# One context loop split in two, two early transposes placed behind the feed-forward, and the loads of c in odd steps, in a fused cross-attention layer

## The chip, the cores and the metric

The kernel runs on one core of a Trainium2 chip. The metric is the device time of one execution in microseconds (us). Before the change it is 1655.78 us, the median of three runs (1654.61 to 1656.57).

## The reference

One transformer layer with cross attention: `x` gives the queries, `c` (the input `ctx_1024`) gives keys and values. Both are 128 sequences of 128 tokens with 256 features, all in 32-bit floating point. There are 16 heads of 16 features. A token attends only to the tokens strictly before it, and the attention row of the first token is set to zero.

```python
q = (query @ Wq + bq).reshape(b, s, N_HEADS, D_K).transpose(0, 2, 1, 3)
k = (key @ Wk + bk).reshape(b, s, N_HEADS, D_K).transpose(0, 2, 1, 3)
v = (values @ Wv + bv).reshape(b, s, N_HEADS, D_K).transpose(0, 2, 1, 3)
scores = jnp.einsum('bhqd,bhkd->bhqk', q, k) / jnp.sqrt(jnp.float32(D_K))
allowed = j < i + mask                     # mask is 0
scores = jnp.where(allowed, scores, NEG_INF)
attn = jax.nn.softmax(scores, axis=-1)
attn = attn.at[:, :, 0, :].set(0.0)
ctx = jnp.einsum('bhqk,bhkd->bhqd', attn, v)
attn_out = ctx @ Wo + bo
x = layer_norm(query + attn_out, ln1_g, ln1_b)
ffn = jax.nn.relu(x @ W1 + b1) @ W2 + b2   # 256 -> 1024 -> 256
out = layer_norm(x + ffn, ln2_g, ln2_b)
```

## The kernel before, in words

The work is cut into 64 pairs of sequences, numbered p = 0 to 63. The instructions of TensorE (PE), VectorE (DVE), ScalarE (ACT) and GpSimd (POOL) stand in the order in which the code emits them. Only the DMA queue of SyncE (SP) is ordered by a planner of the framework, which may place a load ahead of an older transfer. [...]

Pairs 0 and 1 have an order written out by hand. From p = 2 on a loop runs, and this text calls one turn of it a step. Step p does the scores and the softmax of pair p, the context and the output projection of pair p-1, the projections of pair p+1, the transposes of the inputs of pair p+2, and feed-forward work of older pairs. On PE, a step is in this order:

1. `scores(p, 1)`, the high half of the query rows (L333), into two double banks of PSUM. The masks on DVE (L350) read them, and `maximum`, `exponential` and `sums` follow on DVE, POOL and ACT.
2. The first feed-forward unit. A unit is half of the hidden layer (`hidden`, L611) or one sequence of the second layer (`second` at L627, or `second_alone` at L639 with a bank of its own). Each is 16 matrix instructions in the trace, since a 32-bit product is made of two.
3. `scores(p, 0)`, the low half.
4. The second feed-forward unit.
5. `weigh(p-1)`, the context: products of the transposed attention weights `pT` with `vd` (low rows, L443) and `vz` (high rows, L451), 48 products or 96 matrix instructions together. Each writes a strip of 32 partitions, and four strips run side by side. `context` copies the result (ACT, L463).
6. The projections: `queries` (L267), `attention_out` (L470), `keys` (L267), `values` (L299).
7. In steps 2 to 5 `turn_x1_on_pe(p-1)`: four transposes on PE (L233) of the normalised rows `x1` of pair p-1, copied by ACT (L601). From step 6 on `turn_x1` does this with a transpose on DVE (L585) and transfers over DRAM on SP (`across`, L247).
8. The last units. From step 7 on they are both halves of `hidden(p-2)`; steps 2 to 6 take their units from a table, `plan`.

`weigh` needs `pT`. In the loop `turn(p)` makes it: three transposes on DVE (L399), then 16 transfers on the SP queue (L409), each from one block of 32 partitions to another. Blocks 0 and 1 of `pT` belong to the first sequence of a pair and blocks 2 and 3 to the second, so the products of one sequence need 8 of the transfers. PE waits for these through eight semaphores. The framework spreads these waits: it puts four instructions that only wait (two semaphores each but one) ahead of the first product of each sequence, and the last wait sits on that product's weight load itself. The pairs 0, 1 and 63 get `pT` from PE and ACT instead (`turn_on_pe`), without these waits.

`x1` of pair p-1 comes from a chain within step p: the masks, then maxima, sums and transposes on DVE, with POOL and ACT between, then `attention_sum`, the two `tokens` transposes and `norm1` (L508).

PSUM has four single banks for everything but the scores. A new tile takes the bank that was released longest ago, and PE waits until its last reader has finished.

`load` (L92) brings `x` and `c` of two pairs into buffers with four transfers each; `load_tokens` (L99) brings `x` of two pairs once more, by rows. In an even step p the three come for the pairs p+4 and p+5, after `add_bo`. `tokens(p + 2)` reads the loaded buffers in each step (DVE, L252).

Of the kernel before, what the change touches and what calls it, by code (L numbers as in the profile page):

```python
# [13 lines left out]
P = 128  # L14
# [5 lines left out]
def tile_cross_attention_block(  # L20
# [26 lines left out]
    H = 16  # L47
# [6 lines left out]
    NP = B // 2  # L54
# [22 lines left out]

    blocks_of, tokens_of = {}, {}

    def load(ps):  # L80

        n = len(ps)
        for which, src in (("x", x), ("c", c)):
            t = loads.tile(
                [P, KC, n * 2 * NS, 32], F32, tag=f"{which}b{n}", name=f"{which}b_{ps[0]}",
                bufs=n,
            )
            blocks = src[2 * ps[0] : 2 * ps[0] + 2 * n].rearrange(
                "b (i t) (k j f) -> j t k (b i) f", t=32, k=KC, f=32
            )  # L90
            for j in range(NS):
                nc.sync.dma_start(t[32 * j : 32 * j + 32], blocks[j])  # L92
            for u, p in enumerate(ps):
                blocks_of[which, p] = t[:, :, u * 2 * NS : (u + 1) * 2 * NS]

    def load_tokens(g, us=slice(0, 4)):
        if g not in tokens_of:
            tokens_of[g] = loads.tile([P, 4, D], F32, tag="x", name=f"x_{g}")
        nc.sync.dma_start(  # L99
            tokens_of[g][:, us], x[4 * g + us.start : 4 * g + us.stop].rearrange("b p d -> p b d")  # L100
        )
# [118 lines left out]
    def bank(name):  # L220
        return ps_1.tile([P, 512], F32, tag="ps1", name=name)
# [5 lines left out]
    def transposed(src, name):  # L227

        pt = bank(name)
        for k in range(KC):  # L230
            for s in range(2):
                at = (2 * k + s) * P
                nc.tensor.transpose(  # L233
                    pt[:, at : at + P], src[:, s, k * P : (k + 1) * P], ident
                )
        return pt
# [195 lines left out]
    def weigh(p):  # L432

        st = states[p]
        pT = st.pop("pT")
        pc = bank(f"pc_{p}")

        for m in range(KC):
            for s in range(2):
                at = (m * 2 + s) * P  # L440
                blocks = slice(2 * s, 2 * s + 2)
                for j in range(NS):
                    nc.tensor.matmul(  # L443
                        pc[32 * j : 32 * j + 32, at : at + HP],
                        st["vd"][:, s, 4 * m + j].rearrange("p e d -> p (e d)"),
                        pT[:, blocks, H + 2 * j + m, :],
                        start=True, stop=True,
                    )
                for e in range(2):
                    for j in range(NS):  # L450
                        nc.tensor.matmul(  # L451
                            pc[32 * j : 32 * j + 32, at + HP : at + P],
                            st["vz"][:, s, 4 * m + j, 2 * e : 2 * e + 2, :].rearrange(
                                "p e d -> p (e d)"
                            ),
                            pT[:, blocks, 4 * j + 2 * m + e, :],
                            start=(e == 0), stop=(e == 1),
                        )
        st["pc"] = pc
# [133 lines left out]
    def turn_x1_on_pe(p):  # L593
        st = states[p]
        x1T = ffn.tile([P, NS, 4 * 32], F32, tag="x1T", name=f"x1T_{p}")
        st["x1T"] = x1T.rearrange("p i (s k a) -> p s i k a", s=2, k=KC)
        pt = transposed(st["x1"], f"ptn_{p}").rearrange(
            "p (k s i a) -> p k s i a", k=KC, s=2, i=NS
        )
        for k in range(KC):  # L600
            nc.scalar.copy(st["x1T"][:, :, :, k, :], pt[:, k])  # L601

    def hidden(p, fs):
        st = states[p]
        if fs[0] == 0:
            st["hT"] = ffn.tile([P, FC, TP], F32, tag="hT", name=f"hT_{p}")
        for f in fs[::2]:
            ph = bank(f"ph_{p}_{f}")
            for i in range(2):
                for k in range(KC):  # L610
                    nc.tensor.matmul(  # L611
                        ph[:, i * TP : (i + 1) * TP].rearrange("p (s i a) -> p s i a", s=2, a=32),
                        w1[:, k, (f + i) * P : (f + i + 1) * P], st["x1T"][:, :, :, k, :],
                        start=(k == 0), stop=(k == KC - 1),
                    )
            for i in range(2):
                nc.scalar.activation(  # L617
                    st["hT"][:, f + i, :], ph[:, i * TP : (i + 1) * TP], AF.Relu,
                    bias=b1e_c[:, f + i : f + i + 1], scale=1.0,
                )  # L620
# [11 lines left out]
    def second_alone(p, s):  # L632

        st = states[p]
        if "t2" not in st:
            st["t2"] = ffn.tile([P, 2, D], F32, tag="t2", name=f"t2_{p}")
        py = bank(f"py_{p}_{s}")
        for f in range(FC):
            nc.tensor.matmul(  # L639
                py[:, :D], st["hT"][:, f, s * P : (s + 1) * P], w2[:, f, :],  # L640
                start=(f == 0), stop=(f == FC - 1),
            )
        st["py", s] = py
# [27 lines left out]
    def feed(units):  # L671
        for what, p, part in units:
            if what == "hidden":
                hidden(p, range(part * FC // 2, (part + 1) * FC // 2))
            elif p in alone:
                second_alone(p, part)
            else:
                second(p, part)

    def sum_up(units):  # L680

        done = []
        for what, p, part in units:
            if what == "second":
                if p in alone:
                    sum_alone(p, part)
                elif part == 1:
                    second_sum(p)
                if part == 1:
                    done.append(p)  # L690
        return done

    alone = (2, 3)

    def both(what, p):
        return [(what, p, 0), (what, p, 1)]
# [61 lines left out]
    for which in "xc":  # L758
# [9 lines left out]


    plan = {  # L770
        2: ([("hidden", 0, 1)], both("second", 0), both("hidden", 1)),
        3: ([("second", 1, 0)], [("second", 1, 1)], [("hidden", 2, 0)]),
        4: ([("hidden", 2, 1)], [("second", 2, 0)], [("second", 2, 1)]),
        5: ([("hidden", 3, 0)], [("hidden", 3, 1)], [("second", 3, 0)]),
        6: ([("second", 3, 1)], [("hidden", 4, 0)], [("hidden", 4, 1)]),
    }
    waiting, late = [], []
    for p in range(2, NP):
        soon, end = p + 1 < NP, p == NP - 1
        first, then, finally_ = plan.get(  # L780
            p, ([("second", p - 3, 0)], [("second", p - 3, 1)], both("hidden", p - 2))
        )
        scores(p, 1)
        mask(p, 1, 0)
        maximum(p, 1, ONE)
        feed(first)
        mask(p, 1, 1)
        maximum(p, 1, TWO)
        scores(p, 0)
        mask(p, 0, 0)  # L790
        mask(p, 0, 1)
        exponential(p, 1, ONE)
        maximum(p, 0, ALL)
        exponential(p, 1, TWO)
        feed(then)
        sums(p, 1, ONE)
        sums(p, 1, TWO)
        summed = late + sum_up(first + then)
        exponential(p, 0, ALL)
        sums(p, 0, ALL)  # L800
        for q in waiting:
            finish(q)
        weigh(p - 1)
        context(p - 1)
        if soon:
            queries(p + 1)
        attention_out(p - 1)
        if not end:
            turn(p)
        attention_sum(p - 1)  # L810
        if soon:
            keys(p + 1)
        if p + 2 < NP:
            for which in "xc":
                tokens(p + 2, which)
        norm1(p - 1)
        if p > 5:
            turn_x1(p - 1)
        if soon:
            values(p + 1)  # L820
            values_out(p + 1)
        for q in waiting:
            store(q)
        if p <= 5:
            turn_x1_on_pe(p - 1)
        residual1(p - 1)
        for q in summed:
            stats(q, states[q]["t2"], 2)
        if soon:
            add_bo(p + 1)  # L830
        if p % 2 == 0 and p + 4 < NP:
            load([p + 4, p + 5])
            load_tokens(p // 2 + 2)
        for q in summed:
            scale_and_shift(q)
        feed(finally_[:1])
        if end:
            turn_on_pe(p, 1, range(4))
        feed(finally_[1:])
        late = sum_up(finally_)  # L840
        for q in summed:
            norm2(q)
        waiting = summed

    p = NP - 1
# [89 lines left out]
```

## Time and profile before

| What | Value |
|---|---|
| median of three runs | 1655.78 us |
| the profiled execution, its own time | 1652.77 us |
| its span, first to last instruction | 1651.0 us |
| PE busy | 1615.4 us (98%), 16524 matrix instructions |
| DVE, POOL, ACT busy | 1312.6, 1275.4, 766.9 us (80%, 77%, 46%) |
| mean granted clock of TensorE | 0.995 |
| a step in the middle of the run, from scores to scores | 24.77 us |
| the last steps from the table: 3, 4, 5 and 6 | 25.71, 26.67, 26.67, 21.35 us |

An engine's busy time is the time in which one of its instructions ran, as a share of the span. Matrix instructions overlap in the pipeline, so their durations are longer than the distance from one start to the next; distances are what add up to time. `PEld` is the loading of weights, which overlaps with the products. In a timeline each row has its start and its length in us, the engine, the line in the code, the tiles, and in brackets how long the engine had been idle before and what ended that.

### The profile page before, as it was taken

To read this page: it belongs to the slowest core of one execution; us is meant where nothing else is said; L and a number is where in the kernel's file an instruction comes from. 1 tells how busy PE (TensorE), PEld (TensorE's weight loads), DVE (VectorE), ACT (ScalarE), POOL (GpSimd) and SP (SyncE) were. 2 spreads that over 40 slices of the span, in tenths; PEclk is the share of its full clock that TensorE was granted. 3 is DMA by queue.
4 is the path that set the end of the run, shared out by engine and by line. 5 is a ranking of instruction groups with operands and counts; after the bars stand their busy time and mean duration, and the time that the engine had idled before them with its cause. 6 is when DMAs were issued, how large, how long until landed. Compare 5 with 4: busy or idle time off the path is not lost.

```text
span 1651.0 us, 41181 instructions
## 1 busy us (share of the span) xinstructions
PE 1615.4 (98%) x16524; PEld 1342.8 (81%) x16524; DVE 1312.6 (80%) x1983; ACT 766.9 (46%) x1505; POOL 1275.4 (77%) x1108
## 2 busy tenths in 40 slices
PE   7998999999999999999999999999999999999997
PEld 5777888888888888888888888888888888888876
DVE  4767888888888888888888888888888888888852
ACT  4544444444444444444444444444444444444442
POOL 4766878878878878878878878878878878878873
PEclk9999999999999999999999999999999999999999
DMA  8444456566556566655666556565656575556330
GB/s 162 88 104 100 104 138 136 127 151 133 129 128 135 130 148 134 125 133 135 129 146 135 127 130 136 130 146 128 134 134 133 130 149 128 126 134 133 92 87 19
DMA packets 478973, 208.28 MB, mean 126 GB/s; under 512 B 352064, under 2 KB 447296, under 8 KB 478784
## 3 DMA queue, kind: packets, MB, share of 16 engines
q1 hardware_dynamic: 394192, 180.72, 50.3%
q10 hardware_dynamic: 84592, 24.93, 6.2%
q8 instruction: 131, 2.15, 0.6%
q14 instruction: 58, 0.48, 0.1%
HBM read 69.22 MB, written 31.98 MB: 61 GB/s over the span
## 4 chain that ended last, share of the span: by engine, by line
PE 89%; DVE 5%; POOL 3%; issue 1%; DMA 1%; ACT 1%; SPq 1%; ACTq 0%; POOLq 0%; DVEq 0%
PE py L627 25%; PE ph L611 25%; PE pq L267 7%; PE pss L333 7%; PE pk L267 6%; PE pv L299 6%; PE po L470 6%; PE pc L451 3%; PE pc L443 3%; DVE sm L350 1%; DVE nmx L361 1%; POOL sm L383 1%; POOL sm L362 1%; PE py L639 1%; SPq L409 1%
## 5 line engine op out<-in xcount | busy, mean ns | idle before, releaser
L362 POOL TENSOR_TENSOR sm<-sm,nmx 128x1024 f32<-128x1024 f32 x192 | 364.3, 1898 | 219.4 <-DVE nmx L361 219.4
L611 PE MATMUL ph<-x1T,w 128*128 128x256 f32 x2048 | 454.5, 379 | 2.5 <-ACT x1T L601 2.5
L627 PE MATMUL py<-w,hT 128*128 128x256 f32 x1952 | 453.5, 385 | 0.0
L611 PEld LDWEIGHTS ph<-x1T,w 128*128 128x128 f32 x2048 | 388.3, 190 | 57.4 <-ACT x1T L601 3.5
L627 PEld LDWEIGHTS py<-w,hT 128*128 128x128 f32 x1952 | 361.0, 190 | 76.8 <-ACT hT L617 21.9
L350 DVE TENSOR_TENSOR sm<-pss,neg 128x1024 f32<-128x1024 f32 (+1 forms) x256 | 237.9, 950 | 212.6 <-PE pss L333 199.2
L369 ACT ACTIVATE sm<-sm 128x1024 f32<-128x1024 f32 x192 | 203.0, 1057 | 354.0 <-POOL sm L362 344.6
L383 POOL TENSOR_TENSOR sm<-sm,rs 128x1024 f32<-128x1024 f32 x192 | 359.2, 1898 | 2.6 <-DVE rs L382 2.4
L617 ACT ACTIVATE hT<-ph,b1e_c 128x256 f32<-128x256 f32 x512 | 214.1, 470 | 193.5 <-PE ph L611 159.6
L399 DVE STREAM_TRANSPOSE tb<-sm 128x1024 f32<-128x1024 f32 x183 | 220.4, 1231 | 32.2 <-POOL sm L383 22.3
L361 DVE TENSOR_REDUCE nmx<-sm 128x8 f32<-128x1024 f32 (+1 forms) x192 | 234.3, 1220 | 6.6
L381 DVE TENSOR_REDUCE su<-sm 128x8 f32<-128x1024 f32 (+1 forms) x192 | 229.6, 1196 | 1.0 <-ACT sm L369 0.8
L289 ACT ACTIVATE kT<-pk,bkh,half 128x256 f32<-128x256 f32 x256 | 123.6, 563 | 161.7 <-PE pk L267 161.7
L267 PE MATMUL pq<-xT,wq 128*128 128x256 f32 x512 | 130.8, 399 | 3.2 <-ACT xT L669 3.2
L333 PE MATMUL pss<-kT,qT 32*64 32x256 f32 (+1 forms) x4096 | 126.7, 335 | 1.7 <-ACT kT L289 1.3
L470 PE MATMUL po<-wo,cxT 128*128 128x256 f32 x512 | 121.3, 379 | 1.7 <-ACT cxT L463 1.2
L516 POOL TENSOR_TENSOR x1b<-x,g_r 128x512 f32<-128x512 f32 x64 | 81.3, 1271 | 53.7 <-DVE x L508 53.7
L267 PE MATMUL pk<-cT,wk 128*128 128x256 f32 x512 | 121.1, 379 | 1.0 <-ACT cT L669 1.0
L299 PE MATMUL pv<-wv,cT 128*128 128x256 f32 x512 | 121.1, 379 | 0.0
L333 PEld LDWEIGHTS pss<-kT,qT 32*64 32x64 f32 x4096 | 76.3, 131 | 49.1 <-issue 40.6
L267 PEld LDWEIGHTS pq<-xT,wq 128*128 128x128 f32 x512 | 94.2, 194 | 20.3 <-ACT xT L669 3.6
L470 PEld LDWEIGHTS po<-wo,cxT 128*128 128x128 f32 x512 | 97.1, 190 | 15.3 <-ACT cxT L463 1.4
(82 smaller groups left out, 1765.8 us busy)
## 6 DMA issues: line engine op xcount, KB each, us to landing
pT<-tb SPq DMA_DIRECT2D x976, 96.0 KB, 2.2
out_dram<-t ACTq DMA_DIRECT2D x63, 256.0 KB, 3.4
xb<-in_x_dram SPq DMA_DIRECT2D x124, 128.0 KB, 3.8
cb<-in_ctx_dram SPq DMA_DIRECT2D x124, 128.0 KB, 4.7
x<-in_x_dram SPq DMA_DIRECT2D x31, 512.0 KB, 4.7
x1t<-tbx SPq DMA_DIRECT2D x232, 64.0 KB, 1.8
x1T<-x1t SPq DMA_DIRECT2D x58, 256.0 KB, 3.3
vd<-vz ACTq DMA_DIRECT2D x64, 128.0 KB, 2.7
```

The costliest lines, as they stand in the source:

```text
L267: nc.tensor.matmul(ps[:, m * TP : (m + 1) * TP], w[:, k, m * P : (m + 1) * P], src[:, k, :], start=(k == 0), stop=(k == KC - 1),)
L299: nc.tensor.matmul(pv[:, s * D : (s + 1) * D], st["cT"][:, k, s * P : (s + 1) * P], wv[:, k, :], start=(k == 0), stop=(k == KC - 1),)
L333: nc.tensor.matmul(sps[r // 2][s * HP : (s + 1) * HP, r % 2, m * 2 * n : (m + 1) * 2 * n].rearrange("p (e j) -> p e j", e=2), st["qT"][str ...
L350: nc.vector.tensor_tensor(st["sm", hi][:, part, :].rearrange("p (r n) j -> p r n j", r=2), st["sps", hi][t][:, :, : 4 * n].rearrange("p r ...
L361: nc.vector.tensor_reduce(nmx[:, part], sm[:, part, :], AX.X, ALU.max, negate=True)
L362: nc.gpsimd.tensor_tensor(sm[:, part, :], sm[:, part, :], nmx[:, part, None].to_broadcast([P, part.stop - part.start, n]), ALU.add,)
L381: nc.vector.tensor_reduce(su, sm[:, part, :], AX.X, ALU.add)
L383: nc.gpsimd.tensor_tensor(sm[:, part, :], sm[:, part, :], rs[:, :, None].to_broadcast([P, part.stop - part.start, n]), ALU.mult,)
L399: nc.vector.transpose(tb[:, :, at : at + 256].rearrange("p j (n a) -> p n j a", a=32), sm[:, t * 1024 : (t + 1) * 1024].rearrange("p (n j ...
L470: nc.tensor.matmul(po[:, s * D : (s + 1) * D], cxT[:, k, s, :], wo[:, k, :], start=(k == 0), stop=(k == KC - 1),)
L611: nc.tensor.matmul(ph[:, i * TP : (i + 1) * TP].rearrange("p (s i a) -> p s i a", s=2, a=32), w1[:, k, (f + i) * P : (f + i + 1) * P], st[ ...
L627: nc.tensor.matmul(st["py"][:, s * D : (s + 1) * D], st["hT"][:, f, s * P : (s + 1) * P], w2[:, f, :], start=(f == 0), stop=(f == FC - 1),)
```

## The change

There are three parts.

1. In `weigh`, the loop over the two sequences is split. Within each half m of the features, the low products of both sequences come first, then the high products of both. The products and what they accumulate are the same.
2. The table `plan` and the list `alone` are changed, and the PE transposes of `x1` with them. Step 2 ends with one unit instead of two, and steps 3 to 5 have three units as before, moved forward by one. Step 6 has no entry any more and so has four units. In step 2 the PE transpose stays where it was. In steps 3 and 4 it comes behind the last feed-forward unit. From step 5 on (before: step 6) `turn_x1` with DVE and SP is used. The pairs whose second layer has banks of its own are 1 and 2, not 2 and 3.
3. In the loop, `x` is loaded in even steps as before, and `c` of the same two pairs one step later, in the odd step.

```diff
-    def load(ps):
+    def load(ps, both="xc"):
...
-        for which, src in (("x", x), ("c", c)):
+        for which in both:
+            src = x if which == "x" else c
...
                 at = (m * 2 + s) * P
-                blocks = slice(2 * s, 2 * s + 2)
                 for j in range(NS):
                     nc.tensor.matmul(
                         pc[32 * j : 32 * j + 32, at : at + HP],
                         st["vd"][:, s, 4 * m + j].rearrange("p e d -> p (e d)"),
-                        pT[:, blocks, H + 2 * j + m, :],
+                        pT[:, 2 * s : 2 * s + 2, H + 2 * j + m, :],
                         start=True, stop=True,
                     )
+            for s in range(2):
+                at = (m * 2 + s) * P
                 for e in range(2):
                     for j in range(NS):
...
-                            pT[:, blocks, 4 * j + 2 * m + e, :],
+                            pT[:, 2 * s : 2 * s + 2, 4 * j + 2 * m + e, :],
...
-    alone = (2, 3)
+    alone = (1, 2)
...
     plan = {
-        2: ([("hidden", 0, 1)], both("second", 0), both("hidden", 1)),
-        3: ([("second", 1, 0)], [("second", 1, 1)], [("hidden", 2, 0)]),
-        4: ([("hidden", 2, 1)], [("second", 2, 0)], [("second", 2, 1)]),
-        5: ([("hidden", 3, 0)], [("hidden", 3, 1)], [("second", 3, 0)]),
-        6: ([("second", 3, 1)], [("hidden", 4, 0)], [("hidden", 4, 1)]),
+        2: ([("hidden", 0, 1)], both("second", 0), [("hidden", 1, 0)]),
+        3: ([("hidden", 1, 1)], [("second", 1, 0)], [("second", 1, 1)]),
+        4: ([("hidden", 2, 0)], [("hidden", 2, 1)], [("second", 2, 0)]),
+        5: ([("second", 2, 1)], [("hidden", 3, 0)], [("hidden", 3, 1)]),
     }
...
-        if p > 5:
+        if p > 4:
             turn_x1(p - 1)
...
-        if p <= 5:
+        if p == 2:
             turn_x1_on_pe(p - 1)
...
         if p % 2 == 0 and p + 4 < NP:
-            load([p + 4, p + 5])
+            load([p + 4, p + 5], "x")
             load_tokens(p // 2 + 2)
+        if p % 2 == 1 and p + 3 < NP:
+            load([p + 3, p + 4], "c")
...
         feed(finally_[1:])
+        if p in (3, 4):
+            turn_x1_on_pe(p - 1)
         late = sum_up(finally_)
```

## The prediction

> **What bounds the kernel now.** The busy times come first: PE is at 98% of the span, so time can only come from the rest, or from PE time that does no work.
>
> ```profile
> PE 1615.4 (98%) x16524; PEld 1342.8 (81%) x16524; DVE 1312.6 (80%) x1983; ACT 766.9 (46%) x1505; POOL 1275.4 (77%) x1108
> PE 89%; DVE 5%; POOL 3%; issue 1%; DMA 1%; ACT 1%; SPq 1%; ACTq 0%; POOLq 0%; DVEq 0%
> ```
>
> The chain that ended last agrees (second line). Next I cut the first steps at their scores, and set one step from the middle beside them (columns: window, its length, busy time and count of PE, PEld, DVE, ACT, POOL, granted clock, DMA share, GB/s).
>
> ```profile
> 88.36:114.07 25.71, 22.41 (x245) 17.97 (x245) 19.97 (x30) 10.61 (x21) 19.16 (x15) 1.00 0.42 94
> 114.07:140.74 26.67, 23.79 (x246) 19.15 (x245) 18.81 (x26) 11.45 (x23) 19.13 (x16) 0.94 0.44 97
> 140.74:167.41 26.67, 23.79 (x246) 19.12 (x245) 19.91 (x30) 11.43 (x24) 17.33 (x15) 0.94 0.51 108
> 167.41:188.76 21.35, 21.35 (x242) 17.60 (x241) 19.52 (x28) 10.24 (x21) 14.98 (x11) 1.00 0.29 58
> 808.84:833.61 24.77, 24.77 (x257) 20.64 (x256) 20.65 (x31) 11.75 (x23) 19.87 (x18) 1.00 0.51 122
> ```
>
> Steps 3 to 6 all have three units. Step 6 needs 21.35 us, the others 4.4 to 5.3 more, and in steps 4 and 5 the clock is not whole. PE's timeline of step 4 shows why:
>
> ```profile
> 130.13 1.89 PE L299 MATMUL pv<-wv,cT 128*128 128x256 f32 x8
> 134.89 0.88 PE L233 MATMUL ptn<-ident,x 128*128 128x128 f32 x4 [2.88 <-DVE x L508]
> 135.57 5.24 PE L639 MATMUL py<-w,hT 128*128 128x256 f32 x16
> ```
>
> PE waits 2.88 us for `x1`, then a unit takes 5.24 us where it elsewhere takes 3.72. Between 200 and 1560 us no PE product waits for anything by the chain of waits. Still, the context holds a hidden gap. The timelines of pair 1 (`pT` made by PE) and of pair 31 (`pT` by DMA):
>
> ```profile
> 70.47 0.32 PE L443 MATMUL pc<-pT,vd 128*32 128x64 f32 x8
> 70.60 0.41 PE L451 MATMUL pc<-pT,vz 128*32 128x64 f32 x16
> 70.83 0.29 PE L443 MATMUL pc<-pT,vd 128*32 128x64 f32 x8
> 71.95 0.48 PE L267 MATMUL pq<-xT,wq 128*128 128x256 f32 x1
> ```
> ```profile
> 817.97 0.32 PE L443 MATMUL pc<-pT,vd 128*32 128x64 f32 x8
> 818.10 0.41 PE L451 MATMUL pc<-pT,vz 128*32 128x64 f32 x16
> 818.46 0.32 PE L443 MATMUL pc<-pT,vd 128*32 128x64 f32 x8
> 819.60 0.48 PE L267 MATMUL pq<-xT,wq 128*128 128x256 f32 x1
> ```
>
> From the first product to the projection it is 71.95 - 70.47 = 1.48 us without DMA waits and 819.60 - 817.97 = 1.63 with them; all the difference stands ahead of the second low group (0.36 after the first high group, where pair 1 has 0.23). Pair 63, again without waits, has 1.48 too. The 61 contexts with DMA waits exceed 1.48 by 10.9 us in sum, 0.178 each (pair 62's own wait for ACT left out).
>
> **The change part by part.** *Context order.* The records of the waiting instructions show when PE's queue met them. For pair 31 the first four stand at 814.34 to 814.72, 3.6 us ahead of the context; the second four at 818.03, 818.14, 818.25, 818.36, then the weight load with the last wait at 818.43. So a batch costs about 0.40 us. At 818.03, 16 weight loads and 20 products of those ahead had not started; at 814.34 it was 15 and 15. The queue thus ran some 16 pairs of load and product ahead. Now the second batch follows 24 pairs, four at a time in 0.055 us, so a lead of 16 is 0.22 us, and 0.40 - 0.22 = 0.18 stays open, the measured excess. After the change only 8 low pairs stand between the batches. With a lead of 16 the second batch is met while 8 products of the unit before are still to run, 8 x 0.215 = 1.7 us, which hides 0.40. The value is then 61 x 0.178 = 10.9 us. If the cover failed wholly, a batch would cost 0.40 + 0.08 in the open, 61 x (0.48 - 0.18) = 18 us lost: the bounds are -10.9 and +18.
>
> [...] The row shows a gap and a lead near 36 instructions, so I take 10.9.
>
> The waits now also ask for blocks 2 and 3 of `pT` 1.7 us ahead of the context. In the middle of the run the last of the 16 transfers lands at 838.6, the context begins at 842.7: nothing waits.
>
> *First steps.* From the timeline, start to start: high scores 1.05, unit 3.65, low scores 0.77, unit 3.65, context 1.48, projections 7.02, last unit 3.5, transposes 0.68. Step 2 begins unchanged at 57.41, its last unit at 81.26, so step 3 begins at 81.26 + 3.65 = 84.91. Steps 3 and 4 take 21.8 each, step 5 21.2 (no transposes), step 6 24.6 with four units. Step 7 begins at 84.91 + 21.8 + 21.8 + 21.2 + 24.6 = 174.3, against 188.76 before: 14.5 us, of which 0.7 are contexts counted already. 13.7 remain: three waits of 2.84, 2.88, 2.88 (8.6), about 3.2 of half clock, 0.7 for transposes that one pair no longer needs, and the copies that PE waited for.
>
> Is `x1` there in time? From the first mask to its arrival it is 134.89 - 115.26 = 19.63 us (19.62 and 19.63 in steps 3 and 5), and the mask starts 1.2 after the scores: 20.8. PE now comes to the transposes after 1.05 + 3.65 + 0.77 + 3.65 + 1.48 + 7.02 + 3.5 = 21.1. The cover is the last unit, 3.5 us, with 0.3 to spare; without it 3.2 of each wait would be back. Its hidden half reads the copies only after 1.05 us of scores, or later.
>
> Two things eat into this. In step 6 before, DVE took 21.52 us from mask to mask (168.60 to 190.12). Step 5 has the same work, so step 6's masks come 0.4 us late; low scores wait for them: 0.3. And `pT` gets short:
>
> ```profile
> 184.81 12.09 SPq L409 DMA_DIRECT2D pT<-tb  x16
> 837.05 1.99 SPq L244 DMA_DIRECT2D x1t<-tbx  x4
> 842.13 0.38 SPq L247 DMA_DIRECT2D x1T<-x1t  x1
> 843.92 5.11 SPq L92 DMA_DIRECT2D cb<-in_ctx_dram  x4
> ```
>
> The 16 transfers take 10.8 to 12.1 us to issue and 2.2 to land, 13.0 to 14.3. Between transposes and context lie 13.6, 13.6 and 13.3 us in steps 4, 5, 6 (mask + 16.15 to the next step + 9.1): 0 to 1.0 each, I take 0.4. Together 1.5, leaving 12.2.
>
> [...]
>
> *Loads of c.* The same four transfers every second step. In an odd step SP has 16 transfers of `pT` (last one out 28.1 us after the scores), `x1t` 2.0, one of c, the wait for and issue of `x1T` (2.5), three of c: done at about 36, landed at 41 with the 4.7 us of the median. `tokens` reads c in the next step after 24.6 + 19.6 = 44.2. Before, c came a step earlier, with over 25 us to spare; now it is 3. Even steps lose these 5.1 us on SP, where their list ended at 849.75 and the next `pT` began at 851.03. PE sees neither: below by 0, above see the third rival. I take 0.
>
> **Sum.** 12.2 + 10.9 = 23.1 us off the span of 1651.0: 1627.9, own time 1652.77 - 23.1 = 1629.7. The median of the runs is 3.0 above the profiled execution, so 1655.78 - 23.1 = 1632.7.
>
> **The rivals.** (1) *The gap only moves*: the queue doesn't take the context's first loads in while the old unit with another tile shape runs, and the second batch is met in the open. Place: between the two low groups, 61 times, up to +18. For it: PEld is idle 0.33 us before each first L443 group; against it: the first batch is met 3.6 us ahead. Fully open it gives 1655.8 + 18 - 12.2 = 1661.6, slower; it decides over the other parts once a context has more than 0.178 + 12.2/61 = 0.38 us in the open. 5%. (2) *The context gains nothing*, the excess being the waits' own price wherever they stand: 1655.8 - 12.2 = 1643.6. For it: pair 6's excess (0.39) is a true wait for data. 14%. (3) *c comes late*: each us of landing beyond 44.2 delays DVE, which idles 3.2 us a step ahead of the masks, so PE feels it from about 6 us on. At 6.4 us late in 29 steps, 12 us are gone: 1644. Against it: the 4.7 us row. 5%. (4) *The early steps stay*: DVE works 19.5 to 20 us in each, steps of 21.8 leave little, and waits return as late masks, late `pT`, late `x1`. Only 3 of 12 remain: 1655.8 - 10.9 - 3 = 1642. 10%. (5) *Nothing happens*, the parts cancelling: 1655.8. 2%.
>
> **How the numbers follow.** My own case has 64%, at 1632.7, with 1629 to 1637 for its open terms (early waits 0 to 4, contexts 9 to 11). The range reaches to rivals 2 to 4: 1628.5 to 1645. Left out are rivals 1 and 5 and the tails, under 2 in 10. About 0.2% (3.3 us) is what a measurement of this kernel can tell from no change. Faster are cases 2 to 4 and mine, 93%; same 2%; slower 5%.
>
> **What would show it.** In the profile after: contexts of 1.48 us with both low groups 0.1 apart and no gap ahead of the high ones; no wait of L233 for L508 over 0.5 us in steps 3 and 4; no clock under 1.00 between 60 and 1600 us; step 7 at about 174 to 176; steps of 24.6. A gap of 0.3 or more between the low groups shows rival 1, DVE's L252 waiting for c rival 3.

## The result and the profile after

The changed kernel takes 1630.2 us, the median of six runs (1628.72 to 1631.7), beside 1655.67 us for the kernel before, measured with it. The ratio is 0.9847, with a 95% interval of 0.9834 to 0.9859. By this ratio it is 25.3 us faster, by the medians 25.5; the gains below are worked out from the ratios. The forecast was 1632.7, in a range of 1628.5 to 1645.

The profiled execution has a span of 1630.0 us and a time of 1631.7. It lost 2.4 us ahead of step 2, where little was changed: its first scores of pair 2 begin at 59.85, before they began at 57.41. (In other kernels with the same beginning they start between 55.9 and 59.9.) So differences are read from there on.

Busy times and the chain of the page after:

```profile
PE 1602.5 (98%) x16520; PEld 1337.1 (82%) x16520; DVE 1312.8 (81%) x1984; ACT 767.6 (47%) x1503; POOL 1276.6 (78%) x1108
PE 94%; DVE 2%; SPq 1%; POOL 1%; issue 1%; ACT 1%; DMA 1%; ACTq 0%; POOLq 0%; DVEq 0%
```

PE is busy for 12.9 us less; its share of the chain goes from 89% to 94%, and that of DVE from 5% to 2%. The steps 2 to 6 and one from the middle, in the columns used before:

```profile
59.85:87.37 27.52, 25.93 (x261) 20.97 (x261) 19.86 (x30) 11.72 (x24) 20.70 (x17) 1.00 0.24 52
87.37:108.96 21.59, 21.59 (x245) 18.02 (x244) 19.10 (x27) 10.81 (x21) 15.62 (x13) 1.00 0.45 90
108.96:131.11 22.15, 21.80 (x245) 18.10 (x244) 19.65 (x31) 11.04 (x23) 16.54 (x12) 1.00 0.47 107
131.11:152.27 21.16, 21.16 (x242) 17.53 (x241) 19.13 (x28) 11.25 (x23) 18.82 (x18) 1.00 0.53 115
152.27:177.61 25.34, 25.09 (x257) 20.68 (x257) 22.24 (x36) 11.77 (x23) 23.42 (x20) 1.00 0.64 150
802.12:826.73 24.61, 24.61 (x257) 20.56 (x256) 20.64 (x32) 11.77 (x24) 19.90 (x18) 1.00 0.57 127
```

Steps 3 and 5 have no wait of PE left, and the clock is whole. From the scores of step 2 to those of step 7 it is 177.61 - 59.85 = 117.76 us; before it was 188.76 - 57.41 = 131.35. That is 13.6 us. A step in the middle takes 24.61 in place of 24.77. A context from the middle, and the end of step 3, in PE's timeline:

```profile
777.51 0.43 PE L443 MATMUL pc<-pT,vd 128*32 128x64 f32 x16
777.76 0.63 PE L453 MATMUL pc<-pT,vz 128*32 128x64 f32 x32
778.21 0.41 PE L443 MATMUL pc<-pT,vd 128*32 128x64 f32 x16
778.99 0.48 PE L268 MATMUL pq<-xT,wq 128*128 128x256 f32 x1
```
```profile
104.98 3.62 PE L641 MATMUL py<-w,hT 128*128 128x256 f32 x16
108.43 0.60 PE L234 MATMUL ptn<-ident,x 128*128 128x128 f32 x4
108.96 1.12 PE L334 MATMUL pss<-kT,qT 32*64 32x256 f32 x32
```

The context lasts 778.99 - 777.51 = 1.48 us, as long as that of a pair without DMA waits, and the low products of both sequences follow each other without a gap. The transposes follow their unit without a wait. What is left in steps 3 to 6 are late masks in step 6 (its low scores take 1.18 us in place of 0.84) and two late arrivals of `pT`, in steps 4 and 6. In step 4:

```profile
118.08 0.32 PE L443 MATMUL pc<-pT,vd 128*32 128x64 f32 x8
118.75 0.32 PE L443 MATMUL pc<-pT,vd 128*32 128x64 f32 x8 [0.35 <-DMA pT<-tb]
120.12 1.99 PE L268 MATMUL pq<-xT,wq 128*128 128x256 f32 x8
```

That context takes 2.04 us, the one of step 6 takes 1.87.

### The profile page after: what moved, and what is told of

Its sections match the earlier page's. It is cut to its first block, busy times and chain, and to the rows that moved or that the text cites. A ratio compares the mean times of both kernels' runs of the same rounds, so it can differ in the third digit from the quotient of the medians.

```text
span 1630.0 us, 41237 instructions
## 1 busy us (share of the span) xinstructions
PE 1602.5 (98%) x16520; PEld 1337.1 (82%) x16520; DVE 1312.8 (81%) x1984; ACT 767.6 (47%) x1503; POOL 1276.6 (78%) x1108
## 3 DMA queue, kind: packets, MB, share of 16 engines
q8 instruction: 131, 2.15, 0.6%
## 4 chain that ended last, share of the span: by engine, by line
PE 94%; DVE 2%; SPq 1%; POOL 1%; issue 1%; ACT 1%; DMA 1%; ACTq 0%; POOLq 0%; DVEq 0%
PE py L629 26%; PE ph L613 26%; PE pq L268 8%; PE pss L334 7%; PE pk L268 7%; PE po L472 7%; PE pv L300 7%; PE pc L453 3%; PE pc L443 2%; SPq L410 1%; PE py L641 1%; DVE sm L351 1%; DVE nmx L362 0%; PE ptp L426 0%; DMA be_c<-in_L_xattn_ln_b_dram 0%
## 5 line engine op out<-in xcount | busy, mean ns | idle before, releaser
L268 PEld LDWEIGHTS pk<-cT,wk 128*128 128x128 f32 x512 | 98.8, 193 | 14.9 <-ACT cT L671 1.1
```

The costliest lines, as they stand in the source:

```text
L268: nc.tensor.matmul(ps[:, m * TP : (m + 1) * TP], w[:, k, m * P : (m + 1) * P], src[:, k, :], start=(k == 0), stop=(k == KC - 1),)
```

## The experiments

**The parts alone.** Three kernels each make one part of the change to the kernel before. The first has the new order of products in `weigh`:

```diff
                         pT[:, 2 * s : 2 * s + 2, H + 2 * j + m, :],
                         start=True, stop=True,
                     )
+            for s in range(2):
+                at = (m * 2 + s) * P
                 for e in range(2):
```

> The kernel before with the new order in the context alone. My theory (the queue's lead of some 16 pairs of load and product now lies in the unit ahead, and hides the second batch of waits): contexts of 1.48 us in place of 1.64 to 1.68, about 10.5 us faster than before, steps of 24.6. Rival, the waits cost the same wherever they stand: contexts of 1.64, no change. Rival, the gap opens between the two low groups: contexts of 1.9, up to 18 us slower.

Measured: 1644.49 us against 1655.06 for the kernel before, ratio 0.9941 (0.9918 to 0.9964), that is 9.8 us. Contexts take 1.48 us (from 765.30 to 766.78 in the lines below), steps 24.61.

```profile
765.30 0.43 PE L442 MATMUL pc<-pT,vd 128*32 128x64 f32 x16
766.78 0.48 PE L267 MATMUL pq<-xT,wq 128*128 128x256 f32 x1
```

In steps 7 and 8 the contexts took 1.61 and 2.15, since `pT` was late there. The first theory holds. Neither the waits' own price nor a gap between the low groups shows.

The second has the table, the list and the places of the transposes, with the old context and the old loads:

```diff
-    alone = (2, 3)
+    alone = (1, 2)
...
-        if p > 5:
+        if p > 4:
             turn_x1(p - 1)
...
-        if p <= 5:
+        if p == 2:
             turn_x1_on_pe(p - 1)
...
+        if p in (3, 4):
+            turn_x1_on_pe(p - 1)
```

> The kernel before with the table of units and the place of the early transposes changed alone. My theory: the waits of 2.8 us of steps 3 to 5 and the half clock behind two of them are gone, 12 to 13.5 us faster than before, contexts still 1.64. Rival, DVE and the transfers of pT become the limit of steps of 21.8: waits come back as late masks or late pT, only some 3 us faster.

Measured: 1642.09 us, ratio 0.9926 (0.991 to 0.9942), 12.2 us faster. Steps 3 to 5 took 21.77, 21.98 and 21.32 us. But step 6 took 26.57, with a context of 3.27 us that waited 1.6 us for `pT`: the rival is right in this one place.

```profile
161.50 0.32 PE L443 MATMUL pc<-pT,vd 128*32 128x64 f32 x8 [1.59 <-DMA pT<-tb]
```

The third has the loads of c in the odd step:

```diff
-            load([p + 4, p + 5])
+            load([p + 4, p + 5], "x")
             load_tokens(p // 2 + 2)
+        if p % 2 == 1 and p + 3 < NP:
+            load([p + 3, p + 4], "c")
```

> The kernel before with c loaded in the odd step alone. My theory: no engine waits for these loads in either place, within 1 us of before. Rival, c comes late for its transposes on DVE: slower, with waits of the cT transposes for the loads in even steps. Rival, the relief of SP in even steps is worth something: contexts with fewer long gaps, up to 1 us faster.

Measured: 1652.86 us, ratio 0.9986 (0.9977 to 0.9996). At 2.3 us this is more than the 1 us that was expected. The profile doesn't say where from. Steps in the middle take 24.77 as before. The half clock differs from the kernel before (one window of 6.8 us in step 3 and none in step 4), and steps 2 to 6 sum to 132.2 us against 131.35. So what the part is worth by itself stays open.

The parts alone sum to 9.8 + 12.2 + 2.3 = 24.3 us, the whole change gives 25.3. The intervals of the three are 1.6 to 3.8 us wide to each side, so this sum can't show a difference of 1 us.

**The whole change without the third part.** Here x and c are loaded together in even steps, all else is as changed. It was measured twice, the second time beside the unaltered changed kernel.

```diff
-            load([p + 4, p + 5], "x")
+            load([p + 4, p + 5])
             load_tokens(p // 2 + 2)
-        if p % 2 == 1 and p + 3 < NP:
-            load([p + 3, p + 4], "c")
```

> The changed kernel with x and c loaded together in even steps as before. My theory: the short steps 3 to 5 need the transfers of pT soon, and four loads more stand between in even steps; at most 1 us slower than the changed kernel, about 24 us faster than before. Rival, the loads' new place carries a good part of the gain: 5 us or more slower than the changed kernel.

> The changed kernel with x and c loaded together in even steps, again. Its first profile had a context of 4.79 us in step 6, which waits for pT, and a window of half clock behind it. If that is what the loads of c do there, it comes again: step 6 at some 29 us against 25.3, and 2 to 4 us slower than the changed kernel. If it was chance: step 6 at 25 to 26, no difference.

> The changed kernel unaltered, beside the next two on the same chip. 24 to 26 us faster than before, as at first.

Measured: 1631.29 us the first time (ratio to before 0.9862, 0.9845 to 0.9878). The second time it was 1632.62 (0.9872, 0.9859 to 0.9886), beside 1629.43 for the changed kernel (0.9852, 0.9837 to 0.9867). The difference is 3.2 us and the intervals overlap, but the profiles repeat it in one place: step 6 took 29.32 and 28.80 us without the third part, 25.34 and 25.37 with it. Every other step from 2 to 8 agrees within 0.3 us. PE's timeline of step 6, without the third part (second run):

```profile
161.70 0.32 PE L442 MATMUL pc<-pT,vd 128*32 128x64 f32 x8
164.05 0.32 PE L442 MATMUL pc<-pT,vd 128*32 128x64 f32 x8 [2.02 <-DMA pT<-tb]
164.82 1.07 PE L452 MATMUL pc<-pT,vz 128*32 128x64 f32 x32
165.83 3.20 PE L267 MATMUL pq<-xT,wq 128*128 128x256 f32 x8
```

PE waits 2 us for the last of `pT` (2.55 us in the first run), then the projection takes 3.20 us in place of 1.99, in a window of half clock from 164.9 on for 3.4 us. The SP queue shows what came between, first without, then with the third part:

```profile
136.66 1.83 SPq L92 DMA_DIRECT2D xb<-in_x_dram  x2
138.54 3.24 SPq L92 DMA_DIRECT2D cb<-in_ctx_dram  x4
141.88 0.60 SPq L99 DMA_DIRECT2D x<-in_x_dram  x1
148.50 13.78 SPq L409 DMA_DIRECT2D pT<-tb  x16
```
```profile
136.68 3.06 SPq L93 DMA_DIRECT2D xb<-in_x_dram  x3
139.85 0.66 SPq L100 DMA_DIRECT2D x<-in_x_dram  x1
148.52 11.89 SPq L410 DMA_DIRECT2D pT<-tb  x16
```

Both begin to issue `pT` of pair 5 at the same time, but without the third part it takes 13.78 us to issue the 16 transfers (14.31 in the first run), with it 11.89. In the first run the fourth and the fifth of the 16 start 3.2 us apart, the others mostly 0.64. It is not a load of c that the queue waits for there: the last of them has landed at 144.16 us, before the first `pT` is issued at 145.75 (in the second run at 146.07, before 148.50). The waits of the SP queue between 140 and 162 us name another transfer (us in total, times, longest; a line each from the first and the second run without the third part, then all there are with it):

```profile
SPq L409 <- DMA vd<-vz: 2.3, 1, 2.3
SPq L409 <- DMA vd<-vz: 2.0, 1, 2.0
SPq L410 <- DVE tb L400: 7.8, 1, 7.8
SPq L410 <- PE pv L300: 0.4, 1, 0.4
```

`vd<-vz` is a transfer on the queue of ACT. By the traces the framework hands out eight semaphores (counters that a transfer raises when it lands, and that others wait for) to the transfers of both queues in turn: numbers 100 to 107, each with 213 of the 1704 transfers of the kernel before. A transfer waits for the earlier holder of its own to land. In the first run without the third part, the fifth `pT` transfer has the semaphore of `vd<-vz`: that one lands at 150.78, and the fifth starts at 150.80 (in the second run 153.25 and 153.27). With the third part `vd<-vz` has the semaphore of the eighth, lands at 153.41, and the eighth starts at 153.87, without a wait. `vd<-vz` itself is no slower beside the loads of c: from issue to landing it takes 3.85 and 3.57 us without the third part, 3.71 with it. So the four loads of c cost step 6 time because they change which transfers share a semaphore, not because the queue is busy with them. This is read from the trace; no run changes the semaphores alone. That the third part helps step 6 is an accident of this order and no sign of a freer queue: over the whole execution the SP queue waits for `vd<-vz` longer with the third part (103.1 us, 56 times) than in the first run without it (81.3 us, 31 times).

What is shown: the loads of c in the even step cost step 6 about 3.4 to 4 us, once. The step before it is short (21.16 us), so `pT` has no time to spare. In the middle, where steps take 24.61 us, trains of 16 transfers that take up to 14.5 us to issue delay no context in that kernel (1.48 to 1.50 us).

**How far PE's queue runs ahead.** Three kernels change the number of pairs of weight load and product between the two batches of waits: 16, 48 and 12, where the kernel before has 24 and the changed one 8. All else is as changed. `low(m, s)` stands for the low products of feature half m and sequence s, `high(m, s, e)` for half of the high ones; each is 8 pairs.

```diff
-        for m in range(KC):
-            ...
+        low(0, 0), low(1, 0)                    # 16 between
+        low(0, 1), low(1, 1)
+        for m in range(KC):
+            for s in range(2):
+                high(m, s, 0), high(m, s, 1)
```

> The changed kernel with 16 pairs of load and product between the two batches of waits, in place of 8: the low products of both feature halves of the first sequence, then those of the second, then all high products. My theory, a lead of 16 pairs: the second batch is met when the last load of the unit before has started, some 0.5 us ahead of the context, and costs 0.40; so it is just hidden, contexts of 1.48 to 1.55 us, within 4 us of the changed kernel. Rival, the gap grows evenly with the distance (0 at 8, 0.18 at 24): contexts of 1.57, 5 us slower than the changed kernel.

```diff
+        for s in range(2):                      # 48 between
+            for m in range(KC):
+                low(m, s), high(m, s, 0), high(m, s, 1)
```

> The changed kernel with all products of the first sequence ahead of all of the second: 48 pairs between the batches. My theory: the batch is met when 16 pairs are left to run, as with 24 between, so 0.18 us stay open, contexts of 1.65, about 10.5 us slower than the changed kernel. Rival, the gap grows with the distance: 0.4 or more, contexts of 1.9, 25 us slower. Rival, only the change between low and high groups counts: fewer changes, no slower.

```diff
+        low(0, 0), low(1, 0, (0, 1))            # 12 between
+        low(0, 1, (2, 3, 0, 1)), low(1, 0, (2, 3)), low(1, 1)
+        for m in range(KC):
+            for s in range(2):
+                high(m, s, 0), high(m, s, 1)
```

> The changed kernel with 12 pairs of load and product between the batches (the low products of the first sequence and two of its second feature half, then the rest of the low products, then the high ones). With 16 between, the second batch was met 0.02 us after the context began, with 12 pairs waiting. Theory now: ahead of a change of tile shape the queue takes in 12 pairs of the context, no more; with 12 between the batch is met before the context begins and hidden, contexts of 1.48 us, as fast as the changed kernel. Rival: only 8 go in, the batch is met as the context begins, contexts of 1.65 to 1.75, 10 to 15 us slower than the changed kernel.

Measured, with the first waiting instruction of the second batch in us after the context's first product starts (negative: ahead of it; from the records of steps in the middle):

| pairs between | second batch met, us | context, us | median, us | ratio to before |
|---|---|---|---|---|
| 8 (changed) | -2.23 | 1.48 | 1630.2 | 0.9847 (0.9834 to 0.9859) |
| 12 | -1.37 | 1.48 | 1630.04 | 0.9855 (0.9842 to 0.9868) |
| 16 | +0.02 | 1.71 | 1642.78 | 0.9929 (0.9915 to 0.9944) |
| 24 (before) | +0.07 | 1.64 to 1.68 | 1655.67 | 1 |
| 48 | +0.47 | 1.70 | 1644.25 | 0.9935 (0.9918 to 0.9951) |

The row with 24 is the kernel before, without the other parts. Each ratio is to the kernel before as measured beside that kernel. The gap does not grow with the distance, which drops that rival: 0.23 us of excess with 16 and with 48. It does not follow the number of changes between low and high groups either; with 16 these are the fewest, two groups in all:

```profile
756.28 0.88 PE L442 MATMUL pc<-pT,vd 128*32 128x64 f32 x32
756.95 1.10 PE L452 MATMUL pc<-pT,vz 128*32 128x64 f32 x64
757.99 0.48 PE L268 MATMUL pq<-xT,wq 128*128 128x256 f32 x1
```

The low products, which take about 0.47 us in two groups in the changed kernel (0.25 and 0.22), take 756.95 - 756.28 = 0.67. In the kernel with 48 the gap stands where its second sequence begins, at the third low group:

```profile
758.27 0.29 PE L442 MATMUL pc<-pT,vd 128*32 128x64 f32 x8
758.38 0.41 PE L452 MATMUL pc<-pT,vz 128*32 128x64 f32 x16
758.80 0.32 PE L442 MATMUL pc<-pT,vd 128*32 128x64 f32 x8
758.91 0.43 PE L452 MATMUL pc<-pT,vz 128*32 128x64 f32 x16
```

From L452 at 758.38 to the next L442 it is 0.42 us, the others have 0.23. So my expectation for 16 failed: the batch was to be met some 0.5 us ahead, and it was met with 12 pairs of the context waiting. With 12 between it is hidden wholly, as that count says. The edge lies between 12 and 16. With 8 and 12, what is ahead of the batch when it is met adds up to 16 weight loads and 17 products (8 and 9 of the old unit, or 4 and 5, the rest of the context). By the same sum the batch with 16 would have been met when one old product was left, at -2.23 + 8 x 0.215 = -0.51, as I had expected. That it came 0.5 us later, once the first four products of the context had begun, is measured; what holds the queue there is open.

**The place of the early transposes.** The table stays as changed, but in steps 3 and 4 the transposes come ahead of the last unit again.

```diff
-        if p == 2:
+        if p <= 4:
             turn_x1_on_pe(p - 1)
...
-        if p in (3, 4):
-            turn_x1_on_pe(p - 1)
```

> The changed kernel with the transposes of steps 3 and 4 back ahead of the last unit, the table left as changed. My theory: both steps wait for x1 again, 2.8 to 3.2 us each, and the units behind may run at half clock for a window of 3.4 us: 6 us slower than the changed kernel without a window, up to 9.5 with two. Rival, the table itself and not the place of the transposes brought the gain: within 1 us of the changed kernel.

Measured: 1638.93 us, ratio 0.9911 (0.9896 to 0.9926) against 0.9847 with the change. In the profile steps 2 to 6 take 127.2 us, 9.5 more than in the changed kernel. PE's timeline of steps 3 and 4:

```profile
107.66 1.13 PE L234 MATMUL ptn<-ident,x 128*128 128x128 f32 x4 [3.04 <-DVE x L510]
108.59 6.08 PE L641 MATMUL py<-w,hT 128*128 128x256 f32 x16
...
135.42 0.78 PE L234 MATMUL ptn<-ident,x 128*128 128x128 f32 x4 [3.05 <-DVE x L510]
136.04 3.62 PE L641 MATMUL py<-w,hT 128*128 128x256 f32 x16
```

Both waits are back. The first one is followed by two windows of half clock (6.8 us from 106.7 on), the second of equal length by none. The traces show what the difference is. In all 14 of them the changes of the granted clock lie on a grid of 3.413 us, which begins elsewhere in each execution. Cut along that grid, in the columns used before (the window, its length, then PE's busy time; the granted clock is third from the end):

```profile
104.71:108.12 3.41, 1.63 (x8) 1.09 (x6) 3.31 (x8) 2.74 (x7) 2.67 (x4) 1.00 0.25 60
132.02:135.43 3.41, 0.54 (x4) 0.45 (x5) 2.98 (x8) 1.14 (x4) 1.91 (x4) 1.00 0.75 147
135.43:138.84 3.41, 3.41 (x11) 2.75 (x9) 0.00 (x0) 0.65 (x2) 3.33 (x3) 0.50 0.85 227
103.32:106.74 3.42, 1.30 (x7) 0.80 (x5) 3.32 (x8) 2.45 (x7) 2.69 (x4) 1.00 0.27 61
130.63:134.04 3.41, 1.75 (x9) 1.19 (x7) 3.24 (x7) 2.66 (x7) 0.26 (x2) 1.00 0.18 42
161.49:164.90 3.41, 1.39 (x71) 1.04 (x73) 3.33 (x6) 2.00 (x2) 3.41 (x2) 1.00 0.60 145
105.03:108.45 3.42, 1.48 (x7) 0.95 (x6) 3.32 (x8) 2.63 (x7) 2.69 (x4) 1.00 0.25 57
```

The first three lines are the kernel before: its wait in step 3 lies across two windows, the first of them busy for 1.63 us, and full clock follows; its wait in step 4 lies in one window, busy for 0.54 us, and half clock follows. The next two are this kernel's two waits, then come the second run without the third part and the kernel with the new context alone. From step 2 to 1600 us the 14 traces have nine windows of full clock in which PE was busy for 1.39 us or less (idle for 2.02 or more). Each is followed by a window of half clock, and no other window of full clock is; the closest of these is the last line, busy for 1.48 us. So what counted here is how much of a wait falls into one window, not how long it is. A window that was at half clock itself was followed by another with only 0.93 (here) and 1.23 us idle. Ahead of step 2 half clock also follows windows with less idle time (19.38 to 22.79 us in the kernel before, PE busy for all 3.41 us), so this is no more than a reading of this stretch.

The comparison also answers the rival: the place, not the table, brought most of the early steps' gain. Against step 3's 21.59 us in the changed kernel, the wait of 3 us costs 27.75 - 21.59 = 6.2 us with the half clock, and 24.99 - 21.59 = 3.4 in step 4 without.

**A version past the change.** Step 2 too gets its transposes behind its last unit; the table moves one unit from step 2's end to step 3.

```diff
-        2: ([("hidden", 0, 1)], both("second", 0), [("hidden", 1, 0)]),
-        3: ([("hidden", 1, 1)], [("second", 1, 0)], [("second", 1, 1)]),
+        2: ([("hidden", 0, 1)], [("second", 0, 0)], [("second", 0, 1)]),
+        3: ([("hidden", 1, 0)], [("hidden", 1, 1)], both("second", 1)),
...
-        if p == 2:
-            turn_x1_on_pe(p - 1)
...
-        if p in (3, 4):
+        if p in (2, 3, 4):
```

> A version past the change: step 2 too has its transposes behind its last unit. Step 2 then has three units (the second half of hidden 0, both of second 0) and step 3 four (both halves of hidden 1, both of second 1). My theory: the waits of 0.50 and 0.87 us in step 2 go, step 3 takes 25.3, and pT of step 4 gets its time: 1 to 2 us faster than the changed kernel. Rival, DVE's chain of step 2 is the limit, and the wait moves to step 3: no change.

> The version with step 2's transposes behind its last unit, again. Steps 2 to 6 took 116.8 us in its first profile, against 117.8 in the changed kernel: 1 us faster, which five rounds may just tell.

Measured: 1626.83 us (ratio 0.9837, 0.9822 to 0.9851), then 1628.55 (0.9844, 0.983 to 0.9857) beside 1629.43 for the changed kernel (0.9852). The runs can't tell the two apart. The profiles give steps 2 to 6 as 116.75 and 116.73 us, where the changed kernel has 117.76 and 117.61: the waits in step 2 are gone, and in both profiles 0.8 to 0.9 us came back in step 5, where the low scores wait for the masks. It is about 1 us better by the profile alone.

## Why the prediction was right, and where not

- *Context order, 10.9 us.* Right in size, and in mechanism for the order that was chosen. The 60 contexts of pairs 2 to 61 exceed 1.478 by 10.8 us in sum before and by 1.1 after. Of that 1.0 are the late `pT` of steps 4 and 6, so the gap itself gave 10.7 (0.2 of it a true wait for data in step 7 before). The second batch was to be met 1.7 us ahead of the context; it is met 2.23 ahead, with 8 loads and 9 products of the old unit to run. A lead of 16 pairs is not the whole of the mechanism, though: it would have hidden the batch with 16 pairs between too, and that one stood open for 0.23 us. With 16, 24 and 48 pairs between, the runs show the batch in the open, with 8 and 12 hidden, and the part was worth 10.7.
- *First steps, 13.7 gross and 12.2 net.* Right. Without their contexts, steps 2 to 6 got 13.59 - 0.73 + 0.95 = 13.8 us shorter. Step 7 begins 117.8 us after step 2, where 174.3 - 57.4 = 116.9 was worked out and 1.5 set aside. The terms set aside were 0.3 for the low scores behind late masks (step 6: 1.18 in place of 0.84) and 0.4 each for `pT` in steps 4, 5, 6 (0.56, 0, 0.40). The spare 0.3 us of `x1` ahead of the transposes was enough: no wait in steps 3 and 4.
- *The clock.* The half clock behind two of the three waits is gone, as counted. The 3.2 us for it are what the two steps at 0.94 lost, 2 x 26.67 x 0.06. That it was two of three was the chance of one execution: in the kernel with the loads of c alone, which has the same three waits, the profile has three windows of half clock. Between step 2 and 1600 us of the 14 traces, 2.02 us of idle time in one window of 3.41 at full clock were enough, and 1.93 were not. In steps 2 to 6 the changed kernel has no wait of that size at any position of the grid: the two that are closest to each other, in step 2, sum to 0.50 + 0.87 = 1.37 us.
- *Loads of c, 0 us.* This step failed. Its working looked at whether c comes in time, which it does: the last of it is issued about 5 us before DVE reads it, and landed 2.6 us before. It did not look at what the loads do to the other transfers, whose semaphores they shift. And the 0 to 1.0 us for late `pT` was worked out from 10.8 to 12.1 us for the issue of 16 transfers. In the same trace the next such train takes longer, after loads of c, and so does every second one in the middle (12.5 to 14.4 us):

```profile
202.47 2.58 SPq L92 DMA_DIRECT2D cb<-in_ctx_dram  x3
206.41 15.19 SPq L409 DMA_DIRECT2D pT<-tb  x16
```

So the sum had the third part's effect inside without naming it. By the runs it is 3.4 to 4 us in step 6.

- *The rivals.* None came. The gap did not move (rival 1), the context gained (2), c was not late (3), and late masks and late `pT` cost 1.3 us in the early steps, not 9 (4).

The median lies 2.5 us below the forecast. The part that was worked out is closer: in the profiles, the time from the scores of step 2 to the end of the span went from 1651.0 - 57.41 = 1593.6 to 1630.0 - 59.85 = 1570.2 us, which is 23.4 us, where 23.1 was forecast. The other 2 us of the measured gain are as large as the differences between one execution's first 58 us and another's, and no part of the change is tied to them. The forecast also set the median 3.0 us above its profiled execution, as it was before; after the change it lies 1.5 below it (1630.2 and 1631.7). So a part of how close the median came is luck. The clock may have a share in it, which is not shown: of 29 other executions of the kernel before, those with a mean granted clock of 0.996 took 1650.9 to 1652.3 us, and those with 0.992 or 0.993 took 1655.3 to 1658.0.

## What to carry to other kernels

Count the waits in front of an instruction as work of the queue. Here a group of four waiting instructions and one wait on a weight load took about 0.40 us of PE's queue, and it was free only where enough long instructions were still ahead of it (met 2.23 and 1.37 us ahead of the context it was hidden; met 0.02 to 0.47 us after its start the context took 0.16 to 0.23 longer); so put all such groups first, behind the long work. Put a step that needs another engine's late result behind work that doesn't, and read whether the spare time is there from the arrival relative to the stage's start. A transfer that nobody waits for can still matter: here the transfers share eight semaphores in turn, and four loads more ahead of step 6 changed which of them wait for which (29.32 and 28.80 us with them, 25.34 and 25.37 without). So look up what a late transfer waited for before you blame the one ahead of it.

## What was not expected of the hardware

PE's queue met a wait at most some 16 pairs of weight load and product ahead (15 loads and 15 products or 16 and 20 before, 16 and 17 with 8 and 12 pairs between). With 16 pairs of another tile shape it met it only as these began, at +0.02 us, 0.5 us later than the count says; 12 or 8 pairs were no hindrance (-1.37 and -2.23). Waiting instructions in a row stood about 0.11 us apart. And whether half clock followed a wait of PE depended on where it fell on a grid of 3.413 us: a wait of 2.02 us in one window brought it, one of 3.05 us across two did not.
